# A causal attention layer between two routed layers: the first unit's maxima, the third unit's projection and the last unit's exit in another order

## The chip, the cores and the metric

The kernel runs on one core of one Trainium2 chip. The metric is the device time of one launch in microseconds, as the median of several runs. Engines are named as in the profile: PE (TensorE), PEld (its weight loads), DVE (VectorE), ACT (ScalarE), POOL (GpSimd), and SP, whose queue issues most of the transfers.

## The reference

The input `x` has 8 sequences of 1024 tokens of 256 features in float32. A routed feed-forward layer, causal attention of 16 heads of 16 features, and the routed layer again are each added to `x`:

```python
x = x + 0.5 * ffn(layernorm(x))
x = x + attn(layernorm(x))
x = x + 0.5 * ffn(layernorm(x))

# attn
dots = einsum('bhid,bhjd->bhij', q * scale, k)
dots = where(causal, MASK_VAL, dots)
out = einsum('bhij,bhjd->bhid', softmax(dots), v)
return out @ Wo.T + bo

# ffn: each token chooses two of 8 experts
top2_w, top2_idx = top_k(softmax(x @ gate_w.T), 2)
counts = bincount(top2_idx.reshape(-1), length=8)
keep = counts <= cap          # cap = 1280; an expert with more tokens gives nothing
```

An expert that more than 1280 tokens chose adds nothing to any of them. The kernel therefore makes every token's two choices, counts them, and takes the smallest of the eight counts (`fewest`). If even that one is over the capacity, a routed layer adds nothing, and the code of the experts, behind a branch, isn't run. In the execution that is profiled here it isn't run.

## The kernel before

**Units.** `attention` works in 32 units: 8 sequences (`b`) times 4 groups (`g`) of four heads. A unit has two passes over the scores. `m_steps` gives for every query the largest score, without keeping the scores: PE writes scores to a PSUM bank (tiles `sm`), DVE reduces them into `tops[hf]`, one for each half `hf` of the 1024 queries. `settle(u, hf)` turns these maxima on DVE (`turned`), writes them to memory (`top_d`) and reads them back as one more row of each head's q (`qT<-top_d`), so that in the second pass the scores come out with the maximum taken off. `e_steps` is the second pass: scores again, transposed (tiles `sc`), exponentials on ACT (`pT`), for blocks on the diagonal a select on POOL, and `values`, the product with v and a column of ones (`pav`), in two parts.

**Steps.** A unit has 24 steps. In a step the second pass of unit `u` and the first pass of unit `u + 1` alternate on PE. Steps 0 to 7 belong to the first 512 queries (four blocks of 128 keys, `jb`), steps 8 to 23 to the last 512 (eight blocks). The loop begins with `u = -1`, in which unit 0's first pass runs, together with the first eight steps of unit 0's second pass. In unit 0 steps 0 to 7 hold unit 1's first pass only; the scores of the last 512 queries begin in step 8. The last unit has no first pass beside it and takes two steps at a time, that is one block of 128 keys.

**What runs beside the steps.** All else is written as generators that a small planner (`Beside`) advances, at most one piece in a call of `beside.step(kinds)`. A generator yields `PIECE` or `QK` where it next has work for PE, `REST` in the middle of such a piece, which the next call then continues, or a number of calls after which it goes on by itself. The kinds given to `step` are tried in order. These generators matter here:

- `project(u)`: q and k of a unit, kind `QK`. Each half of the tokens is 16 matmul records (`pq`) in two pieces, one activation on ACT (`packed`) and eight transfers on SP (line 845).
- `values_of`: v of 128 tokens (`pv`), two pieces. `weights`: the weights turned (`pt_w`), then the products with the gate's weights (`pt_gc`, whose input `gcs` is made on DVE, `pg`, `pb_v`).
- `prepare(b, wait, apart)`: loads a sequence and takes the statistics of its eight tiles on DVE, after `wait` calls, one every `apart` calls.
- `divided`, `leave_first`, `leave_last`: for the last four groups the products are divided by their sums, multiplied by Wo (`px`) and added to `x`. For the last unit `leave_last` does it without memory: transpose `att_last` (`pt_last`), divide (`normed`), transpose back (`on_last`), copy to `on`, multiply (`px_last`), add, statistics (`ln_stats`).
- `regate`: the choices for the second routed layer: 1/std by a power on POOL (`rstd_g`), the logits, and then `choose`, some twenty small operations on DVE. `fewest` counts, and `either` holds what the branch reads.

**Order.** PE, DVE, ACT and POOL execute in the order in which the code issues (`InOrder`). SP executes in an order that the scheduling fixes when the program is built.

**PSUM.** There are eight banks: six named `score0` to `score5`, asked for in turn by `score()`, and two of `bank()` for everything else. `pav` holds one of the two `bank()` buffers for most of a half.

Of the kernel before, what the change touches and what calls it, by code (L numbers as in the profile page):

```python
# [103 lines left out]
def macaron_kernel(  # L104
# [579 lines left out]
    def attention(run_no, src, dst, gate0, logits, tally):  # L684
# [3 lines left out]
        with stack:  # L688
# [208 lines left out]
            def e_steps(u):  # L897
# [28 lines left out]
                def values(hf, jb, pTs, part):  # L926
                    if jb == 0 and part == 0:
                        pav[hf] = bank(f"pav{u}_{hf}")
# [6 lines left out]
                    else:  # L935


                        cut = 160 if w == 512 else w // 2
                        cols = slice(cut, w) if part else slice(0, cut)
                    for pr in (1, 0):  # L940
                        for h in range(2):
# [3 lines left out]
                                pav[hf][r : r + 32, off + cols.start : off + cols.stop],  # L945
                                vaugs[b % 2][:, jb, v0 : v0 + 32],
                                pTs[pr][:, h, cols],
                                start=(jb == 0 and part == 0),
                                stop=(jb == 4 * hf + 3),
                            )  # L950
                    if u == NU - 1 and jb == 4 * hf + 3:
                        if part == 0:
                            last.append(pav.pop(hf))
                    elif jb == 4 * hf + 3 and part == 0:
                        att = ap.tile([P, 512], F32, tag="att", name=f"att{u}_{hf}", bufs=4)
                        scalar.copy(att, pav.pop(hf))
# [115 lines left out]
            def leave_last(b, hf, pav, copies):  # L1072
                xb = xbs[b]
                att = ap.tile([P, 512], F32, tag="att", name=f"att_last{hf}", bufs=4)
                on = ons[hf]
                normed = ap.tile([P, 4, P], F32, tag="packed", name=f"normed{hf}", bufs=4)
                gpsimd.memset(normed[:, :, : P // 2], 0.0)
                for k in range(2):
                    copies[k](att[:, k * 256 : k * 256 + 256], pav[:, k * 256 : k * 256 + 256])
                yield PIECE  # L1080
                pt = bank(f"pt_last{hf}")
                for i in range(4):
                    transpose(pt[:, i * P : (i + 1) * P], att[:, i * P : (i + 1) * P])
                heads = pt.rearrange("p (i h r) -> p i h r", i=4, h=4)
                inv = ap.tile([P, 4, 4], F32, tag="inv_last", name=f"inv_last{hf}")
                vector.reciprocal(inv, heads[:, :, :, HD])
                for i in range(4):
                    vector.tensor_tensor(
# [7 lines left out]
                for i in range(4):  # L1096
                    transpose(pt[:, i * P : (i + 1) * P], normed[:, i])
# [113 lines left out]
            for u in range(-1, NU):  # L1211
# [43 lines left out]
                for k in range(STEPS) if u < 0 else range(8) if u == 0 else ():  # L1255
# [6 lines left out]
                    if u < 0 and k == 7:  # L1262
                        beside.add(settle(0, 0), first=True)
                        for kT in kTs[2:]:
                            scalar.copy(kT, row16.to_broadcast([P, S]))
# [151 lines left out]
```

## Time and profile before

| | us |
|---|---|
| median of 3 runs (lowest, highest) | 1357.85 (1356.86, 1359.06) |
| profiled execution, its own time | 1351.15 |
| its span in the profile | 1349.4 |
| PE busy | 1309.2 (97%) |
| DVE busy | 1016.4 (75%) |
| ACT busy | 806.7 (60%) |
| POOL busy | 439.8 (33%) |

The times in rows of the profile are microseconds from the span's start, with the duration after them; a bracket at the end of a row says how long the engine had been idle and what it was waiting for. A group `x16` is 16 instructions of one kind one after the other. All compute instructions carry the line of a helper (L37), so rows are told apart by their tiles. Float32 matmuls appear as two records each. The clock that PE was granted (PEclk) is a share of its full speed. All rows come from the profiled execution, which was quicker than the median of the runs, so differences are taken within it.

### The profile page before, as it was taken

What the parts mean: (1) busy time and instruction counts of PE and PEld (TensorE: products, weight loads), DVE (VectorE), ACT (ScalarE), POOL (GpSimd) and SP (SyncE); (2) the same over time, 40 slices, a digit from 0 to 9 for tenths busy, and PEclk for the clock granted to TensorE, in tenths of its full rate; (3) what the DMA queues carried; (4) which work ended last, traced back from release to release, by engine and by line L of the source; (5) the groups of instructions that cost most, each with busy time, mean ns of one, the idle gap of its engine ahead of it and who ended that gap; (6) DMA issues with size and microseconds to landing.
All of it is one profiled execution on the core that took longest, in us unless ns stands there. A gap on an engine that the chain in (4) does not pass through costs nothing.

```text
span 1349.4 us, 51518 instructions
## 1 busy us (share of the span) xinstructions
PE 1309.2 (97%) x20664; PEld 436.6 (32%) x20664; DVE 1016.4 (75%) x3299; ACT 806.7 (60%) x1908; POOL 439.8 (33%) x776
## 2 busy tenths in 40 slices
PE   6799999999999999999999999999999999999994
PEld 2233333333333333333333333333333333333331
DVE  6766677778777787877778777777787777877865
ACT  3346666566666665666666666656566666666562
POOL 3134113542146221452125521354214621143321
PEclk9999999999999999999999999999999999999997
DMA  4101112112211121222122221211221111122201
GB/s 146 41 4 43 43 39 61 58 47 69 59 54 57 53 62 49 61 59 59 51 59 61 58 75 38 62 57 52 65 61 55 55 53 32 48 60 60 64 24 34
DMA packets 67024, 73.73 MB, mean 55 GB/s; under 512 B 24688, under 2 KB 42232, under 8 KB 66776
## 3 DMA queue, kind: packets, MB, share of 16 engines
q1 hardware_dynamic: 65432, 69.56, 17.7%
q8 instruction: 165, 2.70, 0.8%
q10 hardware_dynamic: 1344, 0.79, 0.2%
q14 instruction: 83, 0.68, 0.2%
HBM read 26.87 MB, written 26.20 MB: 39 GB/s over the span
## 4 chain that ended last, share of the span: by engine, by line
PE 94%; DVE 3%; DMA 1%; SPq 1%; issue 1%; ACT 0%; POOL 0%; ACTq 0%; DVEq 0%
PE sc L37 42%; PE pav L37 24%; PE pq L37 8%; PE sm L37 8%; PE pv L37 4%; PE px L37 4%; PE pta L37 1%; SPq L845 1%; DVE first L37 1%; DMA xa<-in_L_attn_x_dram 0%; PE px_last L37 0%; DVE st_g L37 0%; DVE cand_g L37 0%; DVE xa L37 0%; POOL rstd_g L37 0%
## 5 line engine op out<-in xcount | busy, mean ns | idle before, releaser
L37 ACT ACTIVATE pT<-sc 128x512 f32<-128x512 f32 (+3 forms) x1536 | 669.0, 488 | 469.8 <-PE sm L37 353.7
L37 PE MATMUL sm<-kT,qT 32*64 32x512 f32 (+3 forms) x6144 | 726.9, 507 | 0.0
L37 PE MATMUL sc<-qT,kT 32*64 32x512 f32 (+3 forms) x6144 | 695.1, 507 | 8.6 <-DMA qT<-top_d 8.6
L37 POOL TENSOR_SCALAR_AFFINE_SELECT pT<-pT 128x256 f32<-128x256 f32 x512 | 207.6, 407 | 772.6 <-ACT pT L37 765.0
L37 DVE TENSOR_REDUCE first<-sm 128x1 f32<-128x512 f32 x512 | 328.3, 684 | 82.2 <-PE sm L37 66.7
L37 PE MATMUL pav<-pT,vaug 128*32 128x160 f32 (+4 forms) x5120 | 381.9, 370 | 2.8 <-POOL pT L37 2.0
L37 DVE CUSTOM_DVE_ANT_0 sm<-sm,causal 128x256 f32<-128x256 f32 (+3 forms) x512 | 242.2, 516 | 117.9 <-PE sm L37 110.1
L37 DVE CUSTOM_DVE_ANT_0 sm<-sm,causal,first 128x256 f32<-128x256 f32 (+3 forms) x512 | 262.3, 557 | 86.1 <-PE sm L37 74.1
L37 PEld LDWEIGHTS sc<-qT,kT 32*64 32x64 f32 x6144 | 184.3, 130 | 376.9 <-ACT pT L37 303.7
L37 PEld LDWEIGHTS pav<-pT,vaug 128*32 128x32 f32 x5120 | 102.4, 108 | 363.1 <-issue 268.3
L37 PEld LDWEIGHTS sm<-kT,qT 32*64 32x64 f32 x6144 | 203.3, 130 | 14.2 <-issue 4.3
L37 DVE DVE_READ_ACCUMULATOR2_ANT top<- 128x1 f32 x1024 | 145.7, 142 | 0.0
L37 PE MATMUL pq<-xnT,wkqT 128*32 128x512 f32 x1024 | 135.2, 604 | 1.5 <-DVE xnT L37 0.8
L37 PE MATMUL pv<-wvT,xnT 128*32 128x264 f32 x1024 | 80.0, 389 | 1.1 <-ACT wvT L37 0.9
L37 PE MATMUL px<-woT,on 128*32 128x264 f32 x960 | 76.2, 389 | 0.2 <-DVE xa L37 0.2
L37 POOL TENSOR_SCALAR xn_a<-xa,mv_a,rstd_a 128x256 f32<-128x256 f32 x56 | 67.7, 1221 | 0.0
L37 POOL TENSOR_TENSOR xa<-row,xa 128x264 f32<-128x264 f32 x56 | 41.8, 746 | 50.4 <-ACT row L37 50.4
L37 ACT ACTIVATE packed<-pq,bkqT 128x512 f32<-128x512 f32 x64 | 45.4, 709 | 12.3 <-PE pq L37 8.8
L37 POOL TENSOR_TENSOR xa<-xa,bo_all 128x528 f32<-128x528 f32 x32 | 41.3, 1312 | 19.3 <-issue 18.8
L37 PEld LDWEIGHTS pq<-xnT,wkqT 128*32 128x32 f32 x1024 | 25.7, 110 | 55.9 <-issue 50.8
L37 POOL TENSOR_TENSOR on<-on,inv 128x512 f32<-128x512 f32 (+1 forms) x32 | 40.3, 1278 | 9.7 <-DMA inv<-inv_d 9.7
L37 PEld LDWEIGHTS pv<-wvT,xnT 128*32 128x32 f32 x1024 | 29.7, 109 | 26.1 <-ACT att L37 14.1
(125 smaller groups left out, 455.2 us busy)
## 6 DMA issues: line engine op xcount, KB each, us to landing
att_d<-att SPq DMA_DIRECT2D x62, 256.0 KB
qT<-packed SPq DMA_DIRECT2D x256, 32.0 KB
out_dram<-xa SPq DMA_DIRECT2D x16, 512.0 KB
kT<-packed SPq DMA_DIRECT2D x248, 32.0 KB
on<-att_d SPq DMA_DIRECT2D x30, 256.0 KB
inv<-inv_d SPq DMA_DIRECT2D x30, 256.0 KB
xa<-in_L_attn_x_dram SPq DMA_DIRECT2D x7, 1024.0 KB
xa<-in_L_attn_x_dram SPq DMA_DIRECT2D x2, 512.0 KB
```

Source lines behind the costliest of these rows:

```text
L37: i = call(*args, **kwargs)
L845: (nc.scalar if u == 0 and k < 4 else nc.sync).dma_start(out=(kTs, qTs)[k // 4][u % 4][r : r + HD, s0 : s0 + 512], in_=packed[HD * k : HD ...
```

## The change

There are three parts.

1. At the start, `settle(0, 1)` is handed to the planner at step 23 of the opening unit instead of step 1 of unit 0. In unit 0's steps 0 to 7 only `PIECE` work is taken, so `project(2)` begins at step 8 or later. `prepare(1, 10, 1)` takes its statistics later and closer together.
2. In the last unit the products of the last 512 queries go to two banks of 256 queries each. The first bank is complete with block 5, the second with block 7, and each is copied out when it is complete. Both `bank()` buffers are held by them; all that comes beside them asks for `score()` banks.
3. `leave_last` becomes three functions for two tiles of 128 tokens at a time: `turn`, `back` and `leave`. For the first 512 queries they run as `leave_early`, two pieces in each block's step from step 10 on. For the last 512 they stand written out between the last steps, and the choices of the first four tiles (`choosing`) are dealt out between them one by one. The output of the last unit leaves in four transfers of 256 KB instead of two of 512 KB.

```diff
@@ e_steps, values @@
                 def values(hf, jb, pTs, part):
+                    apart = u == NU - 1 and hf == 1
                     if jb == 0 and part == 0:
-                        pav[hf] = bank(f"pav{u}_{hf}")
+                        pav[hf] = [bank(f"pav{u}_{hf}_{k}") for k in range(2 if apart else 1)]
...
-                        cut = 160 if w == 512 else w // 2
+                        cut = 256 - off if apart else 160 if w == 512 else w // 2
                         cols = slice(cut, w) if part else slice(0, cut)
...
-                                pav[hf][r : r + 32, off + cols.start : off + cols.stop],
+                                pav[hf][apart and (part or jb > 5)][r : r + 32, off + cols.start : off + cols.stop],
...
-                                start=(jb == 0 and part == 0),
-                                stop=(jb == 4 * hf + 3),
+                                start=(jb == 0 and (apart or part == 0)),
+                                stop=(jb == 4 * hf + 3 or apart and jb == 5 and part == 0),
                             )
-                    if u == NU - 1 and jb == 4 * hf + 3:
-                        if part == 0:
-                            last.append(pav.pop(hf))
+                    if u == NU - 1:
+                        if jb == 4 * hf + 3 or apart and jb == 5 and part == 0:
+                            if hf not in atts:
+                                atts[hf] = ap.tile([P, 512], F32, tag="att", name=f"att_last{hf}", bufs=4)
+                            for k in range(2) if hf == 0 else (int(jb == 7),):
+                                cols = slice(k * 256, k * 256 + 256)
+                                (scalar.copy if jb == 7 else vector.tensor_copy)(atts[hf][:, cols], pav[hf][k if apart else 0][:, cols])
...
@@ leave_last is replaced @@
+            def leave_last(b, hf, new):
+                xb, on, att = xbs[b], ons[hf], atts[hf]
+                normed = normeds[hf]
+
+                def turn(i):
+                    pt = new(f"pt_last{hf}_{i}")
+                    for k in range(2):
+                        transpose(pt[:, k * P : (k + 1) * P], att[:, (i + k) * P : (i + k + 1) * P])
+                    heads = pt[:, : 2 * P].rearrange("p (i h r) -> p i h r", i=2, h=4)
+                    inv = ap.tile([P, 2, 4], F32, tag="inv_last", name=f"inv_last{hf}_{i}")
+                    vector.reciprocal(inv, heads[:, :, :, HD])
+                    for k in range(2):
+                        vector.tensor_tensor(
+                            normed[:, i + k, P // 2 :].rearrange("p (h d) -> p h d", h=4),
+                            heads[:, k, :, :HD],
+                            inv[:, k].unsqueeze(2).to_broadcast([P, 4, HD]),
+                            ALU.mult,
+                        )
+
+                def back(i, copy):
+                    pt = new(f"on_last{hf}_{i}")
+                    for k in range(2):
+                        transpose(pt[:, k * P : (k + 1) * P], normed[:, i + k])
+                    copy(on[P // 2 :, 1, i * P : (i + 2) * P], pt[P // 2 :, : 2 * P])
+
+                def leave(i):
                     j = hf * HT + i
+                    px = new(f"px_last{hf}_{i}")
                     matmul_cols(px[:, : D + E], on[:, 1, i * P : (i + 1) * P], woT[:, 1, :])
                     vector.tensor_tensor(xb[:, j, :], px[:, : D + E], xb[:, j, :], ALU.add)
                     ln_stats(xb, j, *gate_lns[b])
+                    if i % 2:
+                        nc.sync.dma_start(
+                            out=dst[b, (j - 1) * P : (j + 1) * P].rearrange("(j p) d -> p j d", p=P),
+                            in_=xb[:, j - 1 : j + 1, :D],
+                        )
+
+                return turn, back, leave
+
+
+            def leave_early(b):
+                turn, back, leave = leave_last(b, 0, score)
+                for i in (0, 2):
+                    yield PIECE
+                    turn(i)
+                for i in (0, 2):
+                    yield PIECE
+                    back(i, vector.tensor_copy)
+                for i in range(HT):
+                    yield PIECE
+                    leave(i)
...
@@ the start @@
-                    preparing = beside.add(prepare(1, 2, 2))
+                    preparing = beside.add(prepare(1, 10, 1))
                     projecting = beside.add(project(2))
...
+                    if u < 0 and k == 23:
+                        settling = beside.add(settle(0, 1), first=True)
                     if u == 0 and k == 1:
                         while owed:
                             _, then, part = owed.popleft()
                             then(part)
-                        settling = beside.add(settle(0, 1), first=True)
-                    if u == 0 and k == 7:
+                    if u == 0 and k == 4:
                         beside.finish(settling)
-                    beside.step((QK, PIECE) if u == 0 or not 14 <= k < 20 else ())
+
+                    beside.step((PIECE,) if u == 0 else (QK, PIECE) if not 14 <= k < 20 else ())
@@ the last unit @@
                 for k in range(0, STEPS, 2) if u == NU - 1 else ():
...
+                    if k == 10:
+
+                        for work in leaving:
+                            beside.finish(work)
                     while len(owed) > 2:
                         _, then, part = owed.popleft()
                         then(part)
                     if k == 0:
-                        beside.add(divided(b, 1, 8, 12, ons[1][:, 1], (1, 3, 3, 3)))
+                        beside.add(settle(u, 1), first=True)
+                        dividing_last = beside.add(divided(b, 1, 8, 12, ons[1][:, 1], (1, 3, 3, 3)))
                         beside.add(gate_first(b))
-                    if k == 0:
-                        beside.add(settle(u, 1), first=True)
-                    if k == 8:
+                        normeds = [
+                            ap.tile([P, 4, P], F32, tag="packed", name=f"normed{hf}", bufs=4) for hf in range(2)
+                        ]
+                        for normed in normeds:
+                            gpsimd.memset(normed[:, :, : P // 2], 0.0)
+                    if k == 10:
                         beside.finish(dividing)
-                        copies = (vector.tensor_copy, vector.tensor_copy)
-                        beside.add(chain(leave_last(b, 0, last.pop(), copies), regate(b, 0, HT)), first=True)
-                    for kinds in ((PIECE,), ()):
+                        leaving = [beside.add(leave_early(b), first=True)]
+                    if k == 18:
+                        beside.finish(leaving[0])
+                        beside.finish(dividing_last)
+                    if k == 20:
+                        turn, back, leave = leave_last(b, 1, score)
+
+                        choosing = regate(b, 0, HT)
+                        next(choosing)
+                        if gate0 is not None:
+                            leasts = [fewest("0", gate0[1], score("cnt0"))]
+                    for i in range(2):
                         if light:
                             light.popleft()()
-                        beside.step(kinds)
+                        beside.step((PIECE,))
+                        if (i, k) == (1, 20):
+                            turn(0)
+                            next(choosing)
+                        if (i, k) == (0, 22):
+                            back(0, vector.tensor_copy)
+                            next(choosing)
+                        if (i, k) == (1, 22):
+                            leave(0)
+                            next(choosing)
...
@@ after the last unit @@
-            while beside.open is not None or beside.pending():
+            leave(1)
+            turn(2)
+            next(choosing)
+            next(choosing)
+            back(2, scalar.copy)
+            leave(2)
+            leave(3)
+            while beside.works:
                 beside.step((PIECE,))
-            leasts = [None]
-            for k, _ in enumerate(leave_last(B - 1, 1, last.pop(), (scalar.copy, vector.tensor_copy))):
-                for _ in range((1, 3)[k] if k < 2 else len(beside.works) * STEPS):
-                    beside.step()
-                if k == 1 and gate0 is not None:
-                    leasts = [fewest("0", gate0[1], bank("cnt0"))]
-            drain(regate(B - 1, HT, TB))
-            leasts.append(fewest("1" if gate0 else "1b", tally, bank("cnt1")))
+            rest = regate(B - 1, HT, TB)
+            next(rest)
+            drain(choosing)
+            drain(rest)
+            leasts.append(fewest("1" if gate0 else "1b", tally, score("cnt1")))
```

## The prediction

> **What bounds the kernel now.** I read the page first, then the chain of waits, then the start and the end instruction by instruction.
>
> ```profile
> PE 1309.2 (97%) x20664; PEld 436.6 (32%) x20664; DVE 1016.4 (75%) x3299; ACT 806.7 (60%) x1908; POOL 439.8 (33%) x776
> PE 94%; DVE 3%; DMA 1%; SPq 1%; issue 1%; ACT 0%; POOL 0%; ACTq 0%; DVEq 0%
> ```
>
> TensorE is the chain for 94% of the span, and the middle (100 to 1295 us) has no hole. The change touches none of that, only the two ends. Near 60 us the chain leaves PE. Timeline of SP's queue there, then rows of DVE and PE:
>
> ```profile
> 54.90 0.57 SPq L889 DMA_DIRECT2D top_d<-turned  x1
> 55.57 0.41 SPq L961 DMA_DIRECT2D att_d<-att  x1
> 56.08 3.35 SPq L845 DMA_DIRECT2D kT<-packed  x4
> 59.53 2.44 SPq L845 DMA_DIRECT2D qT<-packed  x4
> 62.07 2.43 SPq L845 DMA_DIRECT2D kT<-packed  x4
> 64.54 2.48 SPq L845 DMA_DIRECT2D qT<-packed  x4
> 67.12 0.53 SPq L891 DMA_DIRECT2D qT<-top_d  x1
> ...
> 50.88 0.15 DVE L37 DVE_READ_ACCUMULATOR2_ANT top<- 128x1 f32 x1
> 54.67 0.21 DVE L37 STREAM_TRANSPOSE turned<-top 128x32 f32<-128x32 f32 x1
> 61.59 0.34 DVE L37 TENSOR_SCALAR gcs<-gsb,g_mean 8x256 f32<-8x256 f32 x1
> 69.06 1.12 PE L37 MATMUL sc<-qT,kT 32*64 32x512 f32 x2 [8.63 <-DMA qT<-top_d]
> ```
>
> The maxima of unit 0's second half are complete at 51.0, but are turned at 54.67 (behind unit 1's first four maxima), and their row of qT stands on SP behind the 16 copies of unit 2's q and k. PE is empty from 60.4 to 69.06. The clock, by windows (the PEclk column follows the five engines):
>
> ```profile
> 66.00:68.00 2.00, 0.00 (x0) 0.00 (x0) 0.00 (x0) 0.00 (x0) 0.00 (x0) 0.50 0.24 53
> 72.00:73.00 1.00, 1.00 (x14) 0.32 (x6) 0.97 (x3) 0.21 (x1) 0.00 (x0) 0.50 0.00 0
> 74.00:75.00 1.00, 1.00 (x18) 0.19 (x10) 0.54 (x2) 0.26 (x2) 0.00 (x0) 1.00 0.00 0
> 1306.00:1307.00 1.00, 0.37 (x3) 0.24 (x3) 0.89 (x3) 1.00 (x3) 0.00 (x0) 1.00 0.01 1
> 1326.00:1327.00 1.00, 0.66 (x3) 0.33 (x3) 0.92 (x5) 0.29 (x1) 0.00 (x0) 0.50 0.00 0
> ```
>
> So the hole also leaves PE at half clock until about 73.6. At the end:
>
> ```profile
> 1306.63 0.77 PE L37 MATMUL pt_last<-ident,att_last 128*128 128x128 f32 x4 [1.20 <-DVE att_last L37]
> 1323.35 0.99 PE L37 MATMUL pav<-pT,vaug 128*32 128x256 f32 x8 [1.24 <-POOL pT L37]
> 1335.37 0.18 DVE L37 BATCH_NORM_AGGREGATE mv_g<-st_g 128x2 f32<-128x6 f32 x1
> 1335.96 1.04 POOL L37 TENSOR_TENSOR rstd_g<-ve_g,half 128x4 f32<-128x4 f32 x1
> 1342.73 0.16 DVE L37 SCALAR_TENSOR_TENSOR either<-least,some 128x1 int32<-128x1 f32 x1
> ```
>
> After PE's last products (1325.9) a serial tail runs to `either`, then 6.5 us to the span's end, which I leave as they are.
>
> **Start: maxima sent at once.** `settle(0, 1)` moves to step 23 of the opening unit: turned at 51.0 to 51.25, `top_d` issued then; the first such pair (29.40, 31.47) has 2.07 us between issues. On SP only `att_d` stays ahead of the second copy: att is copied about 53.5 (53.28+0.58 before, less the 0.4 by which half a pv is shorter than half a pq), so `qT<-top_d` goes at 54.0 and lands 1.81 later (67.12 to 68.93), at 55.8.
>
> **Start: unit 2's q and k later.** Only PIECE work runs in steps 0 to 7: two pv (1.03 each), `turn(wos)` (0.6), pt_gc, pg (1.44). A new wait appears. pt_gc needs `gcs`, made on DVE after unit 1's maxima: 52.11 plus 4 x 0.65, 4 x 0.51, 4 x 0.38 is 58.3, plus 0.93 for the mean and the difference (61.00 to 61.93 before) is 59.2. PE is there at 57.9: its own work would bring it there at 56.7 (60.4 less 3.72 of pq), but the last scores of unit 1's first half need two banks that DVE frees only at 57.5 (two of the third group's four maxima), and run 0.3. Behind pt_gc on PE stand pg and step 8's scores; nobody else waits. pt_gc 0.3, its copy 0.2, pg 1.44: step 8 starts at 61.25 instead of 69.06, 7.8 us earlier, 5.4 us after its row has landed.
>
> Steps 8 to 12 then carry pb_v 1.09, the four pq pieces (1.00, 0.86, 1.00, 0.86), pav 0.41 and 0.73, and five times 0.97 of scores at full clock: 10.8 against 11.6 before (69.06 to 80.69, half of it at half clock). Gain 0.8. The 16 copies go out between about 66 and 77; unit 2's maxima start near 90. Unit 1's first `top_d` row passes between the two groups of eight and has over 10 us. The batch statistics (8 x 0.56 on DVE) now fall in successive steps 10 to 17: 1.29+0.56 = 1.85 per step against PE's 1.78; I charge 0.4. With its old cover (PE's hole) gone that is all they can cost. Start: 7.8+0.8-0.4 = 8.2; as PE's count (hole, slow clock, new wait) gives 7.3, I take 7.9.
>
> **End: same work, other order.** Cuts of 256+256 cost 0.57+0.57, as 0.41+0.73 did: nothing. The two memsets (0.31 each, POOL) move to the last unit's step 0, where POOL has been idle 2.40: nothing. No piece stands in step 8, so the 1.20 wait before pt_last goes; what is late next is ACT (2.07 for four exponentials). Step 8's products end at 1305.43; step 10's fourth group of scores waits for step 8's second exponential (1305.14+2x0.52 = 1306.2) and ends at 1307.3; block 0's products 1.05, two turns 0.35 each: step 12's scores start at 1309.1 (1310.04 before). But steps 10 to 16 now hold two pieces each and take their banks from the six of the scores: the fourth score waits for the fourth exponential two steps back (2.2 us after that group's end), so a step lasts about (5.3+pieces)/2, 3.0 us, where 5.3 is that 2.2, two rows of scores (1.04) and one of products (1.0) and the pieces are 0.6 to 0.9. From 1309.1 to step 18's scores three such steps give 1318.3; scores 0.83 and waiting 0.2, products 1.05: 1320.4, and no piece follows. Before, the same place was passed at 1320.28: the lead is eaten.
>
> Then step 20 (0.65), the products of block 5 (to 1322.15, behind a select), counts 0.3, turn(0), step 22's scores to 1323.3, block 6's products to 1323.9. On POOL the power (0.23+1.04) follows block 6's selects, done 1324.15. DVE's `logits` waits for it, and behind `logits` stands the copy of back(0): 1324.15+0.40+0.22+0.22+0.45 = 1325.45. PE waits 1.2 there, with leave(0) and the last products behind it: these end at 1326.3 or so (1325.9 before). Afterwards DVE is continuous: four choice operations 0.9, addition and statistics 1.1, choices 0.65, 1.1 again, turn(2) 0.6, choices 1.1: 1330.85. Meanwhile back(2) and two px on PE until 1331.7; two more additions with statistics: 1333.9, where 1335.55 stood. The rest (power, choice, count) is as long as before. End: 1.65.
>
> [...] The row: at 1326 the clock is 0.50, although no hole before it exceeds 1.3 us, while the 1.2 us hole at 1305.4 leaves it at 1.00. [...] I take the row: this stretch stays as broken as before. For the 1.3 us wait before pt_gc I take full clock, by the row of 1306.
>
> Unknown: how eight more askers share six banks. Lower bound: each pair costs what an unshared group does, +0.5 us of gain; upper: all four groups serialise to 3.2, 1 us more lost. Output in four transfers instead of two hides behind the 5.9 us choice.
>
> **Sum.** 7.9+1.65 = 9.55: the profiled execution's 1351.15 (span 1349.4) becomes 1341.6. The median of the runs is 1357.85, 6.7 above it; taking the gain from the median: 1348.3.
>
> **Rivals.** (a) The end loses: banks at their dear bound and the clock falling at 58 to 61 too (half clock over pg, about 1.5): 1350 to 1354. For it: nothing in the trace shares score banks. Chance 0.2. (b) Slower: every piece of the last unit waits on DVE as pt_last did. PE is in order, so each 1.2 us stops scores and products alike. There are 16 pieces; past nine the kernel is slower by 0.2% (7.9+2.7 over 1.2); at thirteen 15.6-7.9 = 7.7 more, 1365.5. Against: px_last rows follow their copies without such waits. 0.07. (c) The change doesn't do what it says: SP's order isn't the code's, as `qT<-zeros` at 48.33 shows, and the row still waits. Then PE, out of work 2.1 earlier, loses 2.1 and the end gives 1.65: 1358.3. Against: every copy of computed data stands in code order. 0.05. (d) Better: statistics and pt_gc hide, full clock at the end: 1343 to 1346. 0.08.
>
> **Numbers.** My forecast (1346 to 1351) has 0.6. The range 1344.5 to 1353.5 adds most of (a) and half of (d). About 0.2% (2.7 us) is what a measurement of this kernel can tell from no change. Faster: forecast, (a), (d) 0.88; same (c) 0.05; slower (b) 0.07.
>
> **What would show it.** `turned` on DVE near 51, `qT<-top_d` on SP ahead of all `packed` copies, no 8.63 row, a PE wait of 1 to 2 us before pt_gc, clock 1.00 from 60 to 75, unit 1 some 8 us earlier. At the end groups of 3.0 us, `logits` ahead of back(0)'s copy, last statistics some 1.7 earlier relative to the last unit's start. I am wrong if a wait over 3 us stands before step 8, or if the last unit is longer than before.

## The result and the profile after

| us | before | after |
|---|---|---|
| median of the runs (6 and 6, lowest to highest) | 1355.03 (1351.99 to 1359.06) | 1345.01 (1343.69 to 1345.24) |
| profiled execution, its own time | 1351.15 | 1343.69 |
| its span | 1349.4 | 1342.0 |
| mean granted clock | 0.989 | 0.992 |

The ratio is 0.9917 (95% interval 0.9899 to 0.9935): a gain of 10.0 us in the medians, small but clear of no change, and of only 7.5 between the two profiled executions (7.4 in their spans). The executions of before lie 7 us apart, those of after 1.6; why is a result of its own, below. Of all runs beside the experiments one, of the kernel before, took 3284 us; nothing here explains it, and it is left out. First the page after, the engines' shares and the chain:

```profile
PE 1310.0 (98%) x20664; PEld 436.5 (33%) x20664; DVE 1016.8 (76%) x3301; ACT 806.8 (60%) x1908; POOL 439.8 (33%) x776
PE 95%; DVE 3%; ACT 1%; issue 1%; DMA 0%; POOL 0%; ACTq 0%; DVEq 0%; POOLq 0%
```

PE does the same work in less span, and the DMA and SPq that the chain held are gone. The timeline of SP's queue, DVE's rows and PE's rows where the hole stood (start, duration, engine, line, operation; in brackets the idle time before and its releaser):

```profile
52.07 0.57 SPq L889 DMA_DIRECT2D top_d<-turned  x1
54.08 0.50 SPq L891 DMA_DIRECT2D qT<-top_d  x1
54.67 0.39 SPq L968 DMA_DIRECT2D att_d<-att  x1
...
71.06 3.10 SPq L845 DMA_DIRECT2D kT<-packed  x4
...
51.83 0.21 DVE L37 STREAM_TRANSPOSE turned<-top 128x32 f32<-128x32 f32 x1
59.63 0.34 DVE L37 TENSOR_SCALAR gcs<-gsb,g_mean 8x256 f32<-8x256 f32 x1
...
57.83 1.06 PE L37 MATMUL sm<-kT,qT 32*64 32x128 f32 x16
60.12 0.26 PE L37 MATMUL pt_gc<-ident,gcs 8*128 8x8 f32 x2 [1.23 <-DVE gcs L37]
60.73 0.58 PE L37 MATMUL pg<-gcT,bo_cols 128*128 128x8 f32 x4 [0.35 <-ACT gcT L37]
61.16 1.07 PE L37 MATMUL pg<-gcT,wsb 128*128 128x8 f32 x8
62.16 1.12 PE L37 MATMUL sc<-qT,kT 32*64 32x512 f32 x2
64.11 1.80 PE L37 MATMUL pb_v<-woT,bv_cols 128*128 128x264 f32 x4
```

The small row `qT<-top_d` passes at 54.08, ahead of all sixteen copies, and even ahead of `att_d`. The 8.63 us hole is gone. In its place PE waits 1.23 for `gcs`, and step 8 begins at 62.16. But the scores of step 8 take 1.12, and pb_v 1.80 (0.65 and 1.16 at full clock, in the run filled). The windows (PEclk follows the five engines) say why:

```profile
61.00:62.00 1.00, 1.00 (x11) 1.00 (x10) 0.00 (x0) 0.00 (x0) 0.00 (x0) 1.00 0.07 16
62.00:62.50 0.50, 0.50 (x10) 0.47 (x17) 0.00 (x0) 0.23 (x2) 0.00 (x0) 0.53 0.00 0
62.50:65.00 2.50, 2.50 (x18) 0.79 (x3) 0.76 (x2) 0.77 (x3) 0.00 (x0) 0.50 0.00 0
65.00:66.00 1.00, 1.00 (x11) 0.55 (x18) 0.53 (x1) 0.33 (x1) 0.00 (x0) 0.78 0.00 0
```

The clock fell to one half at 62.03 and came back at 65.45 (a window between 0.50 and 1.00 holds the change, and its share says where). So it fell when the thin stretch was over and the scores of step 8 began. At the end of the kernel, the last unit's exit, by the timeline of DVE and PE:

```profile
1303.35 1.42 PE L37 MATMUL sc<-qT,kT 32*64 32x512 f32 x16
1306.29 1.43 PE L37 MATMUL sc<-qT,kT 32*64 32x512 f32 x16
...
1318.58 0.39 DVE L37 TENSOR_TENSOR logits<-xa,rstd_g 128x32 f32<-128x32 f32 x1 [0.67 <-POOL rstd_g L37]
1319.44 0.43 DVE L37 COPY on<-on_last 64x256 f32<-64x256 f32 x1
1319.93 0.65 PE L37 MATMUL px_last<-woT,on 128*32 128x264 f32 x8 [1.47 <-DVE on L37]
1324.80 1.88 PE L37 MATMUL px_last<-woT,on 128*32 128x264 f32 x16 [0.46 <-ACT on L37]
1327.77 0.18 DVE L37 BATCH_NORM_AGGREGATE mv_g<-st_g 128x2 f32<-128x6 f32 x1
1335.13 0.16 DVE L37 SCALAR_TENSOR_TENSOR either<-least,some 128x1 int32<-128x1 f32 x1
```

Steps of the last unit (two of them shown by their scores) now follow each other 2.9 to 3.5 us apart, `logits` stands ahead of back(0)'s copy and PE waits 1.47 behind both, and the last statistics are complete at 1327.77.

To compare executions I cut each at the same four instructions: the first pv product, unit 1's first scores, the last unit's first scores, and `either`. "Start", "middle" and "end" are the three distances between them.

| us | start | middle | end |
|---|---|---|---|
| before (the first profile) | 73.16 | 1198.13 | 46.80 |
| after | 66.64 | 1198.37 | 44.72 |
| difference | -6.5 | +0.2 | -2.1 |

Together they are 8.4. Of this 0.8 is given back ahead of the first pv (24.61 before, 25.37 after; the executions of all these kernels differ there by up to 1.2) and 0.2 behind `either`, which leaves 7.4.

### The profile page after: what moved, and what is told of

Same layout as the page of the kernel before. It is cut to its first block, busy times and chain, and to the rows that moved or that the text cites. A ratio compares the mean times of both kernels' runs of the same rounds, so it can differ in the third digit from the quotient of the medians.

```text
span 1342.0 us, 51524 instructions
## 1 busy us (share of the span) xinstructions
PE 1310.0 (98%) x20664; PEld 436.5 (33%) x20664; DVE 1016.8 (76%) x3301; ACT 806.8 (60%) x1908; POOL 439.8 (33%) x776
## 4 chain that ended last, share of the span: by engine, by line
PE 95%; DVE 3%; ACT 1%; issue 1%; DMA 0%; POOL 0%; ACTq 0%; DVEq 0%; POOLq 0%
PE sc L37 43%; PE pav L37 25%; PE pq L37 9%; PE sm L37 8%; PE pv L37 4%; PE px L37 4%; PE pta L37 1%; DVE first L37 1%; ACTq L845 0%; DMA xa<-in_L_attn_x_dram 0%; DVE sm L37 0%; PE px_last L37 0%; POOL rstd_g L37 0%; DVE st_g L37 0%; DVE xa L37 0%
## 5 line engine op out<-in xcount | busy, mean ns | idle before, releaser
L37 ACT ACTIVATE packed<-pq,bkqT 128x512 f32<-128x512 f32 x64 | 45.4, 710 | 11.3 <-PE pq L37 5.5
```

The costliest lines, as they stand in the source:

```text
L37: i = call(*args, **kwargs)
```

## The experiments

Each group of kernels was run beside its own runs of before. Their medians: 1357.35 for start_only, settle_only, end_only and gcs_early (18 runs, 1350.92 to 1361.43), 1357.55 for filled, `both`, back_first and power_early (7 runs), 1356.69 for before_a, before_b, undealt and one_bank (9 runs). Ratios are to these runs. "Start" and "end" are of the one profiled execution.

### One part at a time

start_only is before with part 1 of the change alone; end_only is after with the start of before; settle_only moves only the maxima and leaves unit 2's projection in steps 0 to 7:

```diff
@@ settle_only, against before @@
+                    if u < 0 and k == 23:
+                        settling = beside.add(settle(0, 1), first=True)
...
-                        settling = beside.add(settle(0, 1), first=True)
-                    if u == 0 and k == 7:
+                    if u == 0 and k == 4:
                         beside.finish(settling)
@@ start_only has these lines, and @@
-                    preparing = beside.add(prepare(1, 2, 2))
+                    preparing = beside.add(prepare(1, 10, 1))
...
-                    beside.step((QK, PIECE) if u == 0 or not 14 <= k < 20 else ())
+                    beside.step((PIECE,) if u == 0 else (QK, PIECE) if not 14 <= k < 20 else ())
@@ end_only, against after: the lines of start_only taken back @@
```

start_only. 

> The kernel before with part 1 of the change alone: unit 0's second maxima handed over at step 23 of the opening, projection of the third unit from step 8 on, batch statistics from call 10 on. My theory (the gain is two separate gains, of the start and of the end): the start as in the changed kernel, unit 1's step 0 at 91 to 92.5 instead of 97.8, clock near 0.5 from 62 to 65 us, the end as before; 5.5 to 6.5 us faster than before. Rival (the gain needs both parts, or comes from the end): less than 3 us.

settle_only. 

> The kernel before with nothing but unit 0's second maxima handed over at step 23 of the opening; the third unit's q and k stay in unit 0's first steps. My theory (the queue's place of one small row is all; moving the projection is not needed, and it is what brings the wait before pt_gc and the half clock): no wait over 1.5 us before step 8, which starts near 60.5, clock 1.00 throughout, unit 1's step 0 near 87.5; 9 to 11 us faster than before, so better at the start than the changed kernel by 3 to 4. Rival (the row still stands behind the sixteen copies, so both moves are needed): a wait of 5 us or more stays before step 8, and the gain is under 4 us.

end_only. 

> The changed kernel with the start of the kernel before (parts 2 and 3 alone). My theory: the 8.6 us wait at 60 to 69 as before; from the last unit's first scores to the end of the operation that makes the branch's word 44.7 us instead of 46.8; 1.5 to 2.5 us faster than before. Rival (the pieces in the scores' banks cost what the rest gains): no more than 0.5 us either way.

| | median (lowest to highest), us | ratio, 95% | start | end |
|---|---|---|---|---|
| start_only | 1347.27 (1346.67 to 1352.12) | 0.9938 [0.9913, 0.9963] | 68.23 | 46.75 |
| settle_only | 1343.94 (1342.66 to 1347.56) | 0.9908 [0.9882, 0.9933] | 64.21 | 46.72 |
| end_only | 1353.51 (1349.23 to 1359.28) | 0.9975 [0.9956, 0.9994] | 74.7 | 44.9 |

The early maxima alone are worth more than the whole first part, and alone as much as the whole change. In medians the three kernels lie 10.1, 13.4 and 3.8 us below before, each more than was expected of it. For the first two the likely reason is that the expectations were worked out from the first profile of before, while most of its executions are slower (below). SP's queue and PE in settle_only:

```profile
53.45 0.50 SPq L891 DMA_DIRECT2D qT<-top_d  x1
...
54.97 2.44 SPq L845 DMA_DIRECT2D kT<-packed  x4
...
65.44 0.28 PE L37 MATMUL pt_gc<-ident,gcs 8*128 8x8 f32 x2
67.14 0.61 PE L37 MATMUL pg<-gcT,bo_cols 128*128 128x8 f32 x4
```

The row still passes ahead of all sixteen copies, since the copies follow it in the queue as well. And with the projection kept in steps 0 to 7, pt_gc and pg come later, between scores of 512 columns: no wait for `gcs`, PE busy by its records through all of 58 to 90 us, and a clock of 1.00 there. What else part 1 moves, the projection and the batch statistics, therefore costs 66.64 - 64.21 = 2.4 us of the start. The two were not moved singly; the wait and the thin stretch that follow are in the steps which the projection has left.

The end alone gains about 1.9 (46.80 - 44.9), and after has 2.1 of it. The 3.8 in end_only's median is more than its end can give; its start is that of before, and its runs spread as widely (1349.23 to 1359.28).

start_only and after have the same start, but 68.23 and 66.64 us of it: in start_only the clock was at one half for 6.82 us instead of 3.42, as the last section shows.

### Is it the wait for gcs that lets the clock fall?

My first theory: the 1.23 us wait before pt_gc, against the prediction, costs the clock. gcs_early takes it away by making `gcs` on DVE ahead of the two turns (`wvs` and `wos`) that stood before it; the rest is as in after.

```diff
@@ gcs_early, against after: the five DVE lines that make g_mean and gcs @@
         yield PIECE
+        mean = const.tile([E, 1], F32, name="g_mean")
...
+        vector.tensor_scalar(gcs, gsb, mean, None, ALU.subtract)
         turn(wvs, wvT[:, :, :D])
         yield PIECE
         turn(wos, woT[:, :, :D])
-        mean = const.tile([E, 1], F32, name="g_mean")
...
```

> The changed kernel with the mean and difference of the gate's weights (three small operations on DVE that make gcs) moved three planner pieces earlier, so that pt_gc finds its input ready. My theory (the 1.2 us gap before pt_gc, with the thin pg behind it, made the clock fall): no wait before pt_gc, clock 1.00 from 60 to 66, unit 1's step 0 2 to 3 us earlier than in the changed kernel (92.0), 2 to 3 us faster than it. Rival 1 (the clock falls because of pg alone, twelve tiny products of 1.5 us): the wait goes, the clock still falls near 62, 0.5 to 1.2 us faster. Rival 2 (DVE as a whole is what bounds these steps, so the wait moves to another row): under 0.5 us.

Measured: 1343.32 (1342.14 to 1343.81), 0.9898 [0.9874, 0.9922], start 65.46. The wait is gone, and step 8 begins 1.4 us earlier (60.73). But the clock falls all the same, a little earlier. PE's rows, then windows:

```profile
58.68 0.28 PE L37 MATMUL pt_gc<-ident,gcs 8*128 8x8 f32 x2
59.32 0.58 PE L37 MATMUL pg<-gcT,bo_cols 128*128 128x8 f32 x4 [0.35 <-ACT gcT L37]
60.73 0.65 PE L37 MATMUL sc<-qT,kT 32*64 32x512 f32 x2
61.77 2.13 PE L37 MATMUL pb_v<-woT,bv_cols 128*128 128x264 f32 x4
...
58.34:61.75 3.41, 3.06 (x36) 2.01 (x34) 1.68 (x12) 0.46 (x4) 0.00 (x0) 1.00 0.02 5
62.00:64.00 2.00, 2.00 (x12) 1.12 (x20) 1.20 (x3) 0.99 (x2) 0.00 (x0) 0.50 0.00 0
```

In the 3.41 us before the fall PE was busy for 3.06 by its records. The theory has fallen, and rival 1 came true: the wait costs its own time, 1.2 of the start, not the clock.

filled tries the opposite: the wait stays as long as it is, but one dense product is put into it (added work, its result is not read).

```diff
@@ filled, against after @@
+        matmul(bank("pf"), ident, causal)
         pt = bank("pt_gc")
```

> The changed kernel with one dense product (128x128 by 128x512, read by nobody) put on PE into the gap before pt_gc, which it should fill without moving anything else. In the run with gcs early the gap went and the clock still fell at 61.9, so the theory is now: what lets the clock fall is the thin stretch of PE from 57 to 61 us as a whole (scores fed one by one by DVE, transposes, the twelve tiny products of pg), not a wait of a given length. By it the clock stays at 1.00 from 60 to 66 when a third of this stretch is made dense, and the run is 1.0 to 1.8 us faster than the changed kernel. Rival (the tiny products of pg alone make it fall): the clock falls near 62 as before, the same time within 0.5 us, or up to 1 us slower if the filler is late.

Measured: 1343.47 (1341.24 to 1345.59), 0.9909 [0.9882, 0.9936]; in the profiled execution the start is 65.07.

```profile
58.73 1.13 PE L37 MATMUL pf<-causal,ident 128*128 128x512 f32 x2
60.03 0.26 PE L37 MATMUL pt_gc<-ident,gcs 8*128 8x8 f32 x2 [0.17 <-DVE gcs L37]
62.04 0.65 PE L37 MATMUL sc<-qT,kT 32*64 32x512 f32 x2
...
62.00:64.00 2.00, 2.00 (x22) 0.93 (x21) 0.78 (x2) 1.02 (x4) 0.00 (x0) 1.00 0.00 0
```

pt_gc and step 8 stand where they stood in after, but the clock holds, and the start is 1.6 shorter. In this execution, then, 1.13 us of useless work paid for itself. It doesn't always: of the four runs two took 1341.2 and 1341.7 at a mean clock of 0.994, two 1345.3 and 1345.6 at 0.992, which is where all six runs of after lie (0.991 to 0.992); these two have no profile. So in the profiled executions the 2.4 us divide into 66.64 - 65.07 = 1.6 for the clock and 65.07 - 64.21 = 0.9 for the thin stretch itself.

### What before does in an ordinary execution

The first profile of before was one of its quickest executions (1351.15). Two more profiles of the unchanged kernel were taken.

before_a. 

> The kernel before, profiled once more. Its runs spread from 1351 to 1361 us, and the slower ones show a lower mean clock (0.983 against 0.990), while the kernels without the 8.6 us hole stay within 2 or 3 us at 0.991 to 0.994. So the execution profiled first (1351.15, 0.989) was one of its quickest. My theory: in an ordinary run the half clock that the hole brings lasts far longer than to 73.6 us, through most of unit 0, and costs some 6 us there; everything before the hole and after unit 0 as in the first profile. Rival 1: the extra half clock is in the last 30 us. Rival 2: it is spread over the middle, where the hole plays no part.

before_b. 

> The kernel before, profiled a third time, so that at least one profile of an ordinary run (1356 to 1359 us, mean clock 0.983 to 0.986) is had. The same expectations as for the second profile.

They took 1357.38 and 1357.66 at a mean clock of 0.983, like most runs. Middle and end are those of the first profile (1198.46 and 46.79, 1198.42 and 46.91); the start is 77.96 and 78.32 instead of 73.16. before_a's PE at the hole, then the windows behind it:

```profile
69.86 1.12 PE L37 MATMUL sc<-qT,kT 32*64 32x512 f32 x2 [8.24 <-DMA qT<-top_d]
77.75 1.85 PE L37 MATMUL pg<-gcT,wsb 128*128 128x8 f32 x8
...
70.00:75.00 5.00, 5.00 (x42) 1.97 (x43) 2.67 (x6) 2.09 (x4) 0.00 (x0) 0.50 0.00 0
75.00:80.00 5.00, 5.00 (x37) 3.23 (x44) 2.37 (x6) 1.58 (x6) 0.00 (x0) 0.50 0.03 5
80.00:85.00 5.00, 5.00 (x36) 1.71 (x28) 1.72 (x3) 1.08 (x2) 0.04 (x1) 0.50 0.02 3
85.00:90.00 5.00, 5.00 (x72) 1.33 (x56) 3.64 (x8) 2.80 (x6) 3.81 (x3) 0.95 0.01 2
```

The hole is nearly the same (8.24 against 8.63), but the clock stays at one half until 85.5, not 73.2. From the scores at 69.86 that is 15.65 us of PE work at one half, by estimate 7.8 us lost, where the first profile lost (73.23 - 69.06) / 2 = 2.1 (the four records of pb_v took 2.13 at one half in gcs_early, 1.16 at full clock in filled). Measured from the scores behind the hole to unit 1's first scores it is 33.9 us (69.86 to 103.75) against 28.7 (69.06 to 97.77): 5.2 more, close to the estimate's 5.7. Against settle_only's start of 64.21 the hole with its clock costs 13.8 us in before_a and 9.0 in the first profile, half as much again. Both rivals have fallen: middle and end are unchanged.

### The last choices and the two banks

The rest is tried on the version that has settle_only's start and after's end.

```diff
@@ both, against after @@
-                    preparing = beside.add(prepare(1, 10, 1))
+                    preparing = beside.add(prepare(1, 2, 2))
...
-                    beside.step((PIECE,) if u == 0 else (QK, PIECE) if not 14 <= k < 20 else ())
+                    beside.step((QK, PIECE) if u == 0 or not 14 <= k < 20 else ())
@@ back_first, against both: one group of choices (logits to lc_g) from before back(0) to behind turn(2) @@
                             turn(0)
-                            next(choosing)
...
             next(choosing)
             next(choosing)
+            next(choosing)
@@ power_early, against both: POOL's power two steps earlier @@
                         beside.finish(dividing_last)
+                        choosing = regate(b, 0, HT)
+                        next(choosing)
                     if k == 20:
                         turn, back, leave = leave_last(b, 1, score)
-                        choosing = regate(b, 0, HT)
-                        next(choosing)
@@ undealt, against both: no next(choosing) between the steps, and behind the last statistics @@
             next(rest)
-            drain(choosing)
+            drain(regate(B - 1, 0, HT))
             drain(rest)
@@ one_bank, against both: the last 512 products in one bank @@
-                    apart = u == NU - 1 and hf == 1
+                    apart = False
...
-                            turn(0)
...
-                            back(0, vector.tensor_copy)
...
-                            leave(0)
...
+            turn(0)
             turn(2)
+            back(0, vector.tensor_copy)
+            leave(0)
+            leave(1)
```

`both`. 

> The changed kernel with the third unit's projection and the batch statistics back at their old places (of part 1 only the early maxima are kept). My theory (start and end are independent and add up): start as in the run with the maxima alone, end as in the changed kernel; 1340.3 to 1342.3 us, 2 us below the run with the maxima alone, span near 1339. Rival (they do not add up): 1343.5 or more.

back_first. 

> As the run called both, with the copy of back(0) issued on DVE ahead of the logits of the first choices, which wait for POOL's power. My theory (PE's 1.5 us wait before the first px_last of the last 512 queries is that copy standing behind the logits, and the last products stand behind it): the wait goes or falls under 0.5, the last products end about 1 us earlier, 0.7 to 1.3 us faster than both. Rival (from there DVE's own work bounds the end): the wait goes, the end moves by less than 0.3.

power_early. 

> As the run called both, with the power on POOL for the first choices issued at step 18 instead of step 20, ahead of the selects of block 6. Same theory, other remedy: logits at 26.5 us after the last unit's first scores instead of 28.1, selects of block 6 up to 0.5 later; 0.8 to 1.4 us faster than both. Rival (the selects are what the last products wait for): the delay of the selects eats it, within 0.3 of both.

undealt. 

> As the run called both, with the choices of the first four tiles of the last unit not dealt out but made one after the other at the end, ahead of the last four's. My theory (dealing hides some 3.4 us of DVE's small operations and 1.3 us of POOL's power behind waits for PE): the last statistics come 2 to 2.5 us earlier, all the same the end is 2 to 3.5 us later. Rival (DVE bounds the end by its total work, so the order is worth nothing): within 0.7 us of both.

one_bank. 

> As the run called both, with the last 512 queries' products in one bank that is copied out when block 7 is done; turn, back and leave of its first half come after that, the dealt choices stay where they are. My theory (two banks let about 2.1 us of DVE's turning, copying and adding run beside the last two blocks): 1.5 to 2.5 us slower than both. Rival (the wait of 1.5 us behind the logits eats what the first half gains): within 0.5 us.

| | median (lowest to highest), us | ratio, 95% | start | end |
|---|---|---|---|---|
| `both` | 1340.69 (1339.38 to 1342.68) | 0.9885 [0.9860, 0.9910] | 64.20 | 44.48 |
| back_first | 1341.13 (1340.58 to 1342.24) | 0.9887 [0.9864, 0.9910] | 65.76 | 44.08 |
| power_early | 1341.09 (1339.02 to 1342.47) | 0.9886 [0.9861, 0.9912] | 64.21 | 44.33 |
| undealt | 1346.80 (1344.51 to 1349.28) | 0.9934 [0.9915, 0.9952] | 64.21 | 48.44 |
| one_bank | 1342.38 (1341.88 to 1343.98) | 0.9902 [0.9870, 0.9933] | 64.20 | 45.66 |

The parts add up: `both` has settle_only's start (64.21) and, within 0.3, after's end (44.72). It is the best version found: its median lies 16.9 us below that of before beside it, and 4.3 below after's, and its slowest run is below after's quickest, though these two were not run side by side.

Dealing out the choices is worth 48.44 - 44.48 = 4.0, somewhat more than the 2 to 3.5 expected. DVE's rows of undealt:

```profile
1326.19 0.19 DVE L37 TENSOR_TENSOR logits<-xa,rstd_g 128x32 f32<-128x32 f32 x1 [2.82 <-POOL rstd_g L37]
1330.50 0.18 DVE L37 TENSOR_TENSOR logits<-xa,rstd_g 128x32 f32<-128x32 f32 x1
```

The last statistics do come 1.6 earlier than in `both`, but the first four tiles' choices take 4.3 us, and the others' start only behind them, all after these statistics. In `both` the last `logits` starts 38.74 after the last unit's first scores (1326.36), here 42.74. Two banks are worth 45.66 - 44.48 = 1.2, less than the 1.5 to 2.5 expected: in one_bank the first turn waits for the last product, and its px run at half clock (1318.05 to 1324.87).

back_first and power_early both take away most of the 1.5 us that PE waits before leave(0) (0.52 in either), but the end moves by only 0.4 and 0.15 where 0.7 to 1.4 was expected, and the medians don't show even that. (back_first's longer start is not of its edit, which stands at the end: its clock was at one half from 25.17 to 28.58.) PE and DVE of `both`, then of power_early, at the last products:

```profile
1320.82 0.36 DVE L37 TENSOR_TENSOR normed<-pt_last,inv_last 128x64 f32<-128x64 f32 x2
1322.06 1.10 PE L37 MATMUL px_last<-woT,on 128*32 128x264 f32 x16 [0.46 <-ACT on L37]
1322.78 0.43 DVE L37 TENSOR_TENSOR xa<-px_last,xa 128x264 f32<-128x264 f32 x1 [0.62 <-PE px_last L37]
```
```profile
1320.21 0.36 DVE L37 TENSOR_TENSOR normed<-pt_last,inv_last 128x64 f32<-128x64 f32 x2
1321.53 1.99 PE L37 MATMUL px_last<-woT,on 128*32 128x264 f32 x16 [0.46 <-ACT on L37]
1322.70 0.43 DVE L37 TENSOR_TENSOR xa<-px_last,xa 128x264 f32<-128x264 f32 x1 [1.15 <-PE px_last L37]
```

power_early arrives 0.6 earlier at the last `normed` (the last unit begins 0.05 later), and loses it in the next PE piece: its clock fell at 1320.77, ahead of px; in `both` it fell at 1323.14, when px was nearly done. The shorter wait brings some 0.6, but where the clock happens to fall is worth as much. That the clock, and not the order, decides between these three is read from single profiles, not isolated.

## Why the prediction was right and wrong

| step | predicted | in the profile after |
|---|---|---|
| `turned`, `qT<-top_d` issued | 51.0, 54.0 | 51.83, 54.08 |
| wait before pt_gc | 1.3 | 1.23 |
| step 8 | 61.25 | 62.16 (first pv 0.76 later than before) |
| clock from 60 to 75 | 1.00 | 0.50 from 62.03 to 65.45 |
| steps 8 to 12 | 10.8 | 12.7 |
| dearer by batch statistics | 0.4 | 0 (step 13 to unit 1: 17.1 in both profiles) |
| step in the last unit | 3.0 | 3.51, 2.94, 3.25, 2.94 |
| first `logits`, from the last unit's start | 28.25 | 28.20 |
| PE's wait behind it | 1.2 | 1.47 |
| gain at the end | 1.65 | 2.1 |
| gain at the start | 7.9 | 6.5 (quick execution of before), 11.3 (before_a) |

**The mechanism was right, but for the clock.** The hole was a place in SP's queue, it went when the maxima were sent first, the new wait came where it was placed and as long, and at the end the order of `logits` and copy, the wait and the length of steps came out. Rival (b), every piece waiting on DVE, is refuted by an end 2.1 shorter, and (c), the row still waiting, by the row at 54.08. The median came out where rival (d) had it (1343 to 1346), but of its three reasons only the hidden statistics came true: pt_gc did not hide, and the end did not keep its full clock.

Two steps failed, both about the clock and in opposite directions.

**The step that moved the result past the forecast** is the last line of the sum, "taking the gain from the median", with the term under it, a half clock that ends "about 73.6". That was true of the profiled execution, 6.7 below the median; in the two ordinary ones the half clock lasted to 85.5 and 85.7, and the start took 77.96 and 78.32 us instead of 73.16. The gain at the start was 11.3 against before_a where the sum had 7.9: 3.4 too little. The excess of the median over the profile (6.7) was carried over as if the change left it alone; of the 6.2 by which before_a is longer, 4.8 lie in the start, where the hole's half clock is.

**The step that failed within the profiled execution** is "For the 1.3 us wait before pt_gc I take full clock, by the row of 1306". Steps 8 to 12 took 1.9 longer than the sum, of which the half clock is by estimate 3.42 / 2 = 1.7. By itself this would have made the gain smaller than forecast, 6.5 instead of 7.9. Rival (a) had the clock falling there, for 1.5, but put it at pg; all but the last 0.2 us of pg ran at full clock, and the price was paid by scores and pb_v behind it. The row of 1306 was no fit neighbour: that wait stood among scores of 512 columns, this one among matmuls of 8 columns; the last section puts numbers on it. So the point forecast of 1348.3 lies only 3.3 from the result in part by luck: the first error made it too slow, the second too quick.

The length of a gap alone did not tell where the clock fell, at the start or at the end. At the start of after no gap behind 58.62 exceeds 1.23, and in gcs_early none behind 58.33 exceeds 0.35, yet the clock fell. At the end the prediction took 1.65, with this stretch as broken as before: after gained 2.1, and the kernel `both` 46.80 - 44.48 = 2.3. In both of them the clock fell behind gaps of at most 2.11; the late px of `both` (1.10 us, where after's took 1.88) ran at full clock only because it fell later.

**What the change did not need.** The prediction costed the moved projection as part of what removes the hole: "On SP only `att_d` stays ahead of the second copy". settle_only shows that sending the maxima early is enough, and that the rest of part 1 loses 2.4.

## What to carry to other kernels

When a small row unblocks PE, as `qT<-top_d` did behind a hole of 8.63 us here, send it ahead of bulk copies in the queue, and then leave the bulk work where it was: with unit 2's projection kept in steps 0 to 7 PE was busy all through 58 to 90 us, and the start was 2.4 us shorter. Price a hole with the clock behind it, in more than one execution: here the quick profile had 10.24 us at one half, the two ordinary ones 20.48. A wait between thin matmuls is not to be judged by a wait of the same length between dense ones: half clock followed the 1.23 us among matmuls of 8 columns, full clock the 1.20 us among scores of 512.

## What the runs showed of the hardware

**Half clock came in units of 3.41 us.** From 20 to 110 us these stretches stand at one half, read from windows of half a microsecond:

| | clock fell | rose | length, us | over 3.41 |
|---|---|---|---|---|
| before, first profile | 62.99 | 73.23 | 10.24 | 3 |
| before_a | 65.03 | 85.51 | 20.48 | 6 |
| before_b | 65.22 | 85.70 | 20.48 | 6 |
| end_only | 63.44 | 73.68 | 10.24 | 3 |
| end_only, again | 77.09 | 80.50 | 3.41 | 1 |
| start_only | 60.89 | 67.71 | 6.82 | 2 |
| after | 62.03 | 65.45 | 3.42 | 1 |
| gcs_early | 61.75 | 65.16 | 3.41 | 1 |
| back_first | 25.17 | 28.58 | 3.41 | 1 |

settle_only, filled, `both`, power_early, undealt and one_bank have none. The lengths are 1, 2, 3 and 6 times 20.48 / 6 = 3.413, and the next fall lies on the same grid: 1325.92 in before is 370.0 units behind 62.99, 1324.96 in after 370.0 behind 62.03. So the same kernel, with the same hole, paid 3 units in one execution and 6 in two. Where the clock changes differs between executions (it fell at 62.99, 65.03 and 65.22 in the three of before); no run sets that, so its part was not tested by itself.

**Half clock also followed stretches in which PE was never idle.** end_only's second fall, by the 3.41 us before and behind it, then one such stretch of before_a and two of before (first profile):

```profile
73.68:77.09 3.41, 3.41 (x41) 1.98 (x31) 3.03 (x8) 2.23 (x5) 0.00 (x0) 1.00 0.03 5
77.09:80.50 3.41, 3.41 (x27) 1.21 (x27) 1.66 (x4) 1.32 (x4) 0.00 (x0) 0.50 0.03 7
...
71.86:75.27 3.41, 3.41 (x32) 1.17 (x28) 2.94 (x6) 2.34 (x5) 0.00 (x0) 0.50 0.00 0
...
69.81:73.23 3.42, 3.42 (x32) 1.50 (x16) 1.91 (x5) 1.26 (x3) 0.00 (x0) 0.50 0.00 0
73.23:76.64 3.41, 3.41 (x42) 2.07 (x46) 2.93 (x6) 2.35 (x7) 0.00 (x0) 1.00 0.03 5
```

PE's records cover all of each. But end_only's first stretch holds pt_gc and pg, 14 matmul records of 8 columns, with weight loads busy for 1.98 of it. So the busy time of PE does not tell what follows; nor does it in gcs_early (busy for 3.06 of 3.41, then one half) and in filled (2.88 of 3.41 from 58.62 to 62.03, then 1.00).

**Sums over the rows ahead of half and of full clock.** The forms in PE's rows give a measure of density. Count a matmul record as its columns times its share of 128 x 128, the largest form in the rows: `32*64 32x512` counts 512 x 32 x 64 / 16384 = 64, `128*128 128x8` counts 8, `128*128 128x512` counts 512, and a record that a limit cuts counts by its part. Summed over stretches of 3.413 us on the grid that the clock's changes give in each execution:

| stretch | PE busy, us | sum | clock behind it |
|---|---|---|---|
| after 58.62 to 62.03 | 1.83 | 137 | 0.50 |
| gcs_early 58.33 to 61.75 | 3.06 | 1126 | 0.50 |
| end_only 73.68 to 77.09 | 3.41 | 1425 | 0.50 |
| before 69.81 to 73.23 | 3.41 | 1666 | 1.00 |
| before 73.23 to 76.64 | 3.41 | 1500 | 1.00 |
| before_a 71.86 to 75.27, and the next two | 3.41 each | 1169, 945, 1331 | 0.50 |
| before_a 82.10 to 85.51 | 3.41 | 1846 | 1.00 |
| before 1305.44 to 1308.85 (the row of 1306) | 2.22 | 1985 | 1.00 |
| before 1322.50 to 1325.92 (the row of 1326) | 1.76 | 768 | 0.50 |

In these rows half clock stands behind sums of 137 to 1425, full clock behind 1500 and more. In the whole traces of before and after, from their first clock record (15.20 and 17.66) to 1341 us, 761 stretches have full clock behind them, the least sum among them 1500, and 13 half clock, the greatest 976. PE's busy time does not part them, as the table shows. The sums were read off the traces afterwards, for this kernel's float32 matmuls, and no run was made to test them.

They give an estimate of why it was 3 units in one execution and 6 in another. In before a limit of the grid lies 0.75 us after PE had begun again (69.81 and 69.06), and the stretch from there held scores alone, 1666. In before_a it lies 2.0 after (71.86 and 69.86); that stretch already held pt_gc, the next ones pg, and at half clock three in a row came to 1169, 945 and 1331. filled has no change of clock from 20 to 110 us, so its grid is not known there: the added product is 1024, and between after's limits it would have made 137 + 1024 = 1161 by estimate, which stands among the sums with half clock behind them. Whether that is why two of its four runs were no quicker than after was not shown.
